# Output projection moved behind all of attention, with two levels of seven products, and projections per 512 tokens

## The chip, the cores and the metric

One core of a Trainium2 chip runs the whole kernel; the other cores are idle. The metric is the device time of one execution in microseconds (us), as a median of several runs. Everything is computed in float32.

## The reference, cut to what matters

A layer of a transformer for 1024 tokens of width 512: attention, then a feed-forward part with a small router, each between a layer norm before and a layer norm behind, with the input added again.

```python
q = (hidden_states @ w_q).reshape(B, S, Hkv, g, D)      # 512 -> 32 heads of 128
k = (hidden_states @ w_k).reshape(B, S, Hkv, D)         # 512 -> 8 heads of 128
v = (hidden_states @ w_v).reshape(B, S, Hkv, D)
scores = jnp.einsum('bqhgd,bkhd->bhgqk', q, k) * scale  # causal mask, softmax over k
attn = jnp.einsum('bhgqk,bkhd->bqhgd', probs, v)
return attn.reshape(B, S, Hq * D) @ w_o                 # 4096 -> 512
...
x = x + _layernorm(_L0_attn_ref(_layernorm(x), ...))
x = x + _layernorm(_L0_ffn_ref(_layernorm(x), ...))
```

The feed-forward part multiplies by a 512 x 512 base matrix, and by eight small matrices of rank 16 that are weighted by a softmax over 15 routes.

## The kernel before, in words

Tokens are cut into 8 row tiles of 128 (`t` from 0 to 7). The 8 key heads are 8 groups (`g`), each with 4 query heads (R). A **block** is one (g, t), 64 in all; the list `blocks` (lines 88 to 92) sets their order: for groups 0 to 5 t from 0 to 7, while the last two groups go in turn over pairs of row tiles, in the order 0, 3, 2, 1.

One turn of the main loop (lines 1212 to 1286) is one block `i`. TensorE's order is the order in which the program issues it, four quarters a block. Each quarter has
- `scores` (line 701): the products of 32 queries x 4 heads with all keys up to the diagonal, into one of two PSUM buffers `s`. VectorE adds the mask and takes the minimum (line 720), ScalarE takes the exponential with its sum (735), VectorE the reciprocal (745), ScalarE scales (746), VectorE turns 32 x 32 squares of the result into the tile `T` (752);
- a share of other TensorE work: the product `po` of weights and values of block i-2 (`weighted_values`, 777), the output projection of an earlier pair of blocks, and the projections of queries, keys and values that come next.

Between the turn and `po` stands `to_keys` (767): when the four quarters of `T` are there, 16 DMAs (4 heads x 4 quarters) move it into `K`, with the keys on the partitions. They are issued by SyncE, in some short blocks by SyncE and GpSimd. SyncE also issues nearly every load; a queue takes its DMAs in order.

Projections use seven products in place of eight for a 2 x 2 block product (sums of blocks by GpSimd in lines 181 to 248, merging of results by VectorE in `merge`, lines 561 and 609, and `add`, 539). Queries of a pair of row tiles (256 tokens) are 28 products of 128 columns (`project_q_halves`, 542). Keys and values of a pair are 14 each of 128 columns for two groups at once (`project_halves`, 603). The first group's queries, keys and values are partly done in full (`project_q`, `project_k`, `project_v`). In the list of groups, such a product is named by its result: `pq`, `pk`, `pv`.

The output projection of a pair (`project_o_pair`, 823) is 14 products of 256 columns, one level of seven products, added by VectorE to the running sums `acc` in SBUF (line 858) after every group. Its results are `pa` to `pe`. For the last group it is done row by row in full (`project_o`, 796, result `pO`), so that norms, router and base layer of finished rows (`ffn_norms`, `ffn_router`, `ffn_out`, 884 to 1015) fill later blocks. After the last block the rest of the rows follows in an order written out by hand (lines 1289 to 1324).

Of the kernel before, what the change touches and what calls it, by code (L numbers as in the profile page):

```python
# [10 lines left out]
I32 = mybir.dt.int32  # L11
# [11 lines left out]
def kernel(  # L23
# [17 lines left out]

# [6 lines left out]
    KC = H // P  # L63
    QB = 512
    NQB = S // QB
    TPB = QB // P
    PQ = 2 * P
# [6 lines left out]
    RANK = ER // E  # L74
    scale = float(D) ** -0.5
# [7 lines left out]
    ffn = ctx.enter_context(tc.tile_pool(name="ffn", bufs=2))  # L83
# [3 lines left out]

    pairs = [(g, u) for g in range(G - 2) for u in range(NT // 2)]
    pairs += [(g, u) for u in (0, 3, 2, 1) for g in (G - 2, G - 1)]
    blocks = [(g, 2 * u + e) for g, u in pairs for e in range(2)]  # L90
    N = len(blocks)
    N2 = (G - 2) * NT


    QL = range(N2 // 2 + 5, N // 2)
    QW = [*range(1, N2 // 2 + 4), *QL]
# [3 lines left out]

    def order(ins):

        return keep(ins)
# [9 lines left out]

    def turn_tile(kind, g, t):

        if (kind, t % 2) in long_tiles:
            return long_tiles[kind, t % 2]
        size = (NT - 1 + t % 2) * NSUB * P
        w = turn.tile([P, size], F32, tag=f"{kind}{t % 2}", name=f"{kind}_{g}_{t}")
        if (g, t) in blocks[N2 + 6 : N2 + 8]:  # L120
            long_tiles[kind, t % 2] = w
        return w

    def spare(kind, e, n):

        at = (NT - 3 + e + n) * NSUB * P
        return long_tiles[kind, e][:, at : at + NSUB * P].rearrange("p (k n) -> p k n", k=KC // 2)

    def last_sums(m):

        g, u = pairs[m]
        w = [weights["q", i][1] for i in range(2)]
        hk = KC // 2
        a11, a12, a21, a22 = w[0][:, :hk], w[0][:, hk:], w[1][:, :hk], w[1][:, hk:]
        s1, s2, s4 = spare("T", 0, 0), spare("T", 0, 1), spare("T", 1, 0)
        xp = xnT[u * PQ // QB][:, :, ts(u % (QB // PQ), PQ)]
        b11, b12, b21, b22 = xp[:, :hk, :P], xp[:, :hk, P:], xp[:, hk:, :P], xp[:, hk:, P:]
        t1, t2, t3, t4 = (spare("K", 0, n // 2)[:, :, ts(n % 2, P)] for n in range(4))
        todo = [
            (s1, a21, a22, ALU.add),  # L140
            (s2, s1, a11, ALU.subtract),
            (a21, a11, a21, ALU.subtract),
            (s4, a12, s2, ALU.subtract),
        ]
        if weights["tx of"] != u or m == QL[0]:
            todo += [
                (t1, b12, b11, ALU.subtract),
                (t2, b22, t1, ALU.subtract),
                (t3, b22, b12, ALU.subtract),
                (t4, b21, t2, ALU.subtract),  # L150
            ]
        weights["sq", 0] = (a11, a12, s4, a22, s1, s2, a21)
        weights["sq"] = (g,)
        weights["tx"] = (b11, b21, b22, t4, t1, t2, t3)
        weights["tx of"] = u
        return todo

    long_tiles = {}

    LATE = {(e, n): k for e, ks in enumerate(((0, 0, 2, 2), (4, 0, 0, 0))) for n, k in enumerate(ks)}  # L160

    weights = {}

    def load_k(g, by=nc.scalar):
        wk = wp.tile([P, KC * D], F32, tag="wk", name=f"wk_{g}")
        wk = weights["k", g] = wk.rearrange("p (c n) -> p c n", c=KC)
        load(wk, w_k[:, ts(g, D)].rearrange("(c p) n -> p c n", p=P), by)

    def scale_k(g):
        keep(nc.scalar.mul(weights["k", g], weights["k", g], scale))  # L170

    def load_q(g, i, by=nc.scalar):

        if weights.get(("q", i), (None,))[0] == g:
            return
        hw = R * D // 2
        w = wp.tile([P, KC, hw], F32, tag=f"wq{i}", name=f"wq_{g}_{i}", bufs=1)
        load(w, w_q[:, ts(2 * g + i, hw)].rearrange("(c p) n -> p c n", p=P), by)
        weights["q", i] = (g, w)

    pool_jobs = []

    def pool_off(most):

        for _ in range(min(most, len(pool_jobs))):
            pool_jobs.pop(0)()
# [4 lines left out]
    def combine_w(key, parts, sums):  # L191


        (a11, a12, a21, a22), (s1, s2, s4) = parts, sums
        for dst, p, q, op in (
            (s1, a21, a22, ALU.add),
            (s2, s1, a11, ALU.subtract),
            (a21, a11, a21, ALU.subtract),
            (s4, a12, s2, ALU.subtract),
        ):  # L200
            pool_sum(dst, p, q, op)
        weights[key] = (a11, a12, s4, a22, s1, s2, a21)

    def combine_q(m):

        g = pairs[m][0]
        if weights.get("sq", (None,))[0] == g:
            return
        w = [weights["q", i][1] for i in range(2)]
        hk = KC // 2  # L210
        parts = w[0][:, :hk], w[0][:, hk:], w[1][:, :hk], w[1][:, hk:]
        sums = [
            ffn.tile([P, hk, 2 * D], F32, tag="hy", name=f"sq_{g}_{n}", bufs=3) for n in range(3)
        ]
        combine_w(("sq", 0), parts, sums)
        weights["sq"] = (g,)

    def combine_k(g):

        w = [weights["k", n] for n in (g, g + 1)]  # L220
        hk = KC // 2
        two = ffn.tile([P, 2, hk, D], F32, tag="hT", name=f"sk_{g}")
        kv = ffn.tile([P, KC, NR + ER], F32, tag="skv", name=f"skv_{g}", bufs=1)
        kv = kv.rearrange("p c n -> p (c n)")[:, : 2 * hk * D]
        kv = kv.rearrange("p (x c n) -> p x c n", x=2, c=hk)
        weights["skv"] = kv[:, 1]
        parts = w[0][:, :hk], w[0][:, hk:], w[1][:, :hk], w[1][:, hk:]
        combine_w(("sk", g), parts, (two[:, 0], two[:, 1], kv[:, 0]))

    def combine_v(gv):  # L230

        hk = KC // 2
        two = ffn.tile([P, 2, hk, D], F32, tag="hT", name=f"sv_{gv}")
        w = [weights["v", gv, i * hk, "half"] for i in range(2)]
        parts = w[0][:, :, :D], w[1][:, :, :D], w[0][:, :, D:], w[1][:, :, D:]
        combine_w(("sv", gv), parts, (two[:, 0], two[:, 1], weights.pop("skv")))

    def combine_x(u, m):

        hk = KC // 2  # L240
        xp = xnT[u * PQ // QB][:, :, ts(u % (QB // PQ), PQ)]
        b11, b12, b21, b22 = xp[:, :hk, :P], xp[:, :hk, P:], xp[:, hk:, :P], xp[:, hk:, P:]
        t12, t34 = (ffn.tile([P, 2, hk, P], F32, tag="x", name=f"tx_{u}_{m}_{n}") for n in range(2))
        t1, t2, t3, t4 = t12[:, 0], t12[:, 1], t34[:, 0], t34[:, 1]
        for dst, p, q in ((t1, b12, b11), (t2, b22, t1), (t3, b22, b12), (t4, b21, t2)):
            pool_sum(dst, p, q, ALU.subtract)
        weights["tx"] = (b11, b21, b22, t4, t1, t2, t3)
        weights["tx of"] = u

    def load_v(gv, i, by=nc.scalar):  # L250

        w = wp.tile([P, KC // 2 * GV * D], F32, tag="wv", name=f"wv_{gv}_{i}")
        w = w.rearrange("p (c n) -> p c n", c=KC // 2)
        rows = w_v[ts(i, KC // 2 * P), ts(gv, GV * D)]
        load(w, rows.rearrange("(c p) n -> p c n", p=P), by)
        weights["v", gv, i * (KC // 2), "half"] = w
        for c in range(KC // 2):
            weights["v", gv, i * (KC // 2) + c] = w[:, c, :]

    def load_o(g, by=nc.scalar):  # L260
        wo = wp.tile([P, R, H], F32, tag="wo", name=f"wo_{g}")
        for j in range(R):
            load(wo[:, j, :], w_o[ts(g * R + j, P), :], by)
        weights["o", g] = wo

    def load_base(tag, cs, by=nc.scalar):
        for c in cs:
            w = weights["base", c] = wp.tile([P, H], F32, tag=tag, name=f"wbase_{c}")
            load(w, base_wt[ts(c, P), :], by)

# [13 lines left out]
    load_k(0, nc.sync)  # L284
    for i in range(2):
        load_q(0, i, two[1 - i])
    for t in range(TPB, NT):
        load(x_in[:, t, :], x[ts(t, P), :])

    ident = const.tile([P, P], F32, tag="ident", name="ident")  # L290
    make_identity(nc, ident)
    diag = ffn.tile([P, P], F32, tag="hwT", name="diag")
    neg_half = const.tile([P, 1], F32, tag="neg_half", name="neg_half")
    nc.gpsimd.memset(neg_half, -0.5)

    xnT = [big.tile([P, KC, QB], F32, tag=f"xnT{b}", name=f"xnT_{b}") for b in range(NQB)]


    hn = H // 2
    sums_o = [big.tile([P, 5, hn], F32, tag=f"acc{u}", name=f"acc_{u}") for u in range(NT // 2)]  # L300
    acc = [
        sums_o[t // 2][:, 1 + 2 * (t % 2) : 3 + 2 * (t % 2), :].rearrange("p a n -> p (a n)")
        for t in range(NT)
    ]


    late = {}
# [27 lines left out]

    def prepare_map():

        emap_f = const.tile([P, NR], F32, tag="emap_f", name="emap_f")
        keep(nc.vector.tensor_copy(emap_f, emap_i))
        for e in range(E):  # L340
            keep(
# [1024 lines left out]
```

## Time and profile before

| what | value |
|---|---|
| median of 3 runs | 1051.4 us (1051.25 to 1052.24) |
| the profiled execution, its own time | 1052.36 us |
| span of its records | 1050.6 us |
| mean granted TensorE clock | 0.999 |
| transfers | 112.02 MB in 79668 packets, mean 107 GB/s |
| `K<-T` transfers issued by SyncE | 969 (507, 589, 1847 ns to issue: least, median, most) |
| `K<-T` from issue to landing | 1.7, 2.1, 6.3 us (least, median, most) |

How to read it: the profile has busy time, count and mean duration for groups of instructions by line, engine and tile; PE is TensorE, DVE VectorE, ACT ScalarE, POOL GpSimd, SP SyncE; SPq is SyncE's issuing of DMAs. A group is named "result <- operands". Helpers record the instructions, so all products stand under line 106 and are told apart by their tiles. In a row of the timeline the columns are start, duration, engine, line, operation, tiles, shapes and how many were merged. A row by windows has the window, its length, then busy time and count for TensorE, its weight load, VectorE, ScalarE and GpSimd, the granted clock, the share of the DMA engines' time and GB/s.

### The profile page before, as it was taken

To read this page: it belongs to the slowest core of one execution; us is meant where nothing else is said; L and a number is where in the kernel's file an instruction comes from. 1 tells how busy PE (TensorE), PEld (TensorE's weight loads), DVE (VectorE), ACT (ScalarE), POOL (GpSimd) and SP (SyncE) were. 2 spreads that over 40 slices of the span, in tenths; PEclk is the share of its full clock that TensorE was granted. 3 is DMA by queue.
4 is the path that set the end of the run, shared out by engine and by line. 5 is a ranking of instruction groups with operands and counts; after the bars stand their busy time and mean duration, and the time that the engine had idled before them with its cause. 6 is when DMAs were issued, how large, how long until landed. Compare 5 with 4: busy or idle time off the path is not lost.

```text
span 1050.6 us, 16002 instructions
## 1 busy us (share of the span) xinstructions
PE 1042.0 (99%) x4974; PEld 736.8 (70%) x4974; DVE 720.8 (69%) x1855; ACT 471.9 (45%) x962; POOL 287.8 (27%) x524
## 2 busy tenths in 40 slices
PE   9999999999999999999999999999999999999997
PEld 7876677767787677667787667767788555666554
DVE  4676557776577766776477765876567867577676
ACT  2654435553344544554245444654234654444422
POOL 5413015341030214341031312542162112333112
PEclk9999999999999999999999999999999999999999
DMA  5145332653125352453314442464332773543331
GB/s 190 32 126 146 71 91 71 169 150 85 26 55 161 92 122 67 117 153 79 76 51 122 109 108 69 128 171 118 86 108 89 180 183 91 141 120 92 83 97 41
DMA packets 79668, 112.02 MB, mean 107 GB/s; under 512 B 18704, under 2 KB 51200, under 8 KB 79584
## 3 DMA queue, kind: packets, MB, share of 16 engines
q1 hardware_dynamic: 76592, 106.79, 39.2%
q0 software_dynamic: 1904, 2.90, 1.2%
q10 hardware_dynamic: 1088, 1.31, 0.4%
q8 instruction: 40, 0.66, 0.3%
q14 instruction: 44, 0.36, 0.1%
HBM read 33.34 MB, written 2.10 MB: 34 GB/s over the span
## 4 chain that ended last, share of the span: by engine, by line
PE 97%; DVE 1%; ACT 1%; issue 1%; POOL 0%; DVEq 0%; ACTq 0%; POOLq 0%
PE po L106 23%; PE s L106 21%; PE pq L106 19%; PE pv L106 5%; PE pk L106 5%; PE pe L106 5%; PE pa L106 5%; PE pf L106 3%; PE pO L106 3%; PE pb L106 2%; PE pc L106 2%; PE pd L106 2%; PE pl L106 1%; PE idle L109 1%; DVE s L720 0%
## 5 line engine op out<-in xcount | busy, mean ns | idle before, releaser
L746 ACT ACTIVATE p<-p,rec 128x32 f32<-128x32 f32 (+31 forms) x256 | 188.2, 735 | 269.6 <-DVE rec L745 269.5
L106 PE MATMUL po<-K,v 128*128 128x512 f32 x576 | 279.7, 594 | 0.3
L106 PE MATMUL s<-kT,qT 128*128 128x512 f32 (+15 forms) x768 | 272.0, 463 | 0.0
L752 DVE STREAM_TRANSPOSE T<-p 128x128 f32<-128x128 f32 (+7 forms) x256 | 198.3, 776 | 64.8 <-ACT p L746 49.5
L720 DVE CUSTOM_DVE_ANT_0 s<-s,smask 128x32 f32<-128x32 f32 (+31 forms) x256 | 180.3, 704 | 88.4 <-PE s L106 87.9
L735 ACT ACTIVATE p<-s,nmax 128x32 f32<-128x32 f32 (+31 forms) x256 | 178.9, 699 | 129.2 <-DVE nmax L720 126.6
L106 PEld LDWEIGHTS s<-kT,qT 128*128 128x128 f32 x768 | 140.0, 190 | 111.0 <-issue 100.7
L699 POOL MEMSET p<- 128x96 f32 (+2 forms) x192 | 29.1, 152 | 537.9 <-DVE T L752 492.1
L106 PEld LDWEIGHTS po<-K,v 128*128 128x128 f32 x576 | 103.7, 190 | 59.4 <-issue 50.4
L540 DVE TENSOR_TENSOR qT<-pq,qT 128x256 f32<-128x256 f32 x180 | 80.2, 461 | 44.9 <-ACT qT L566 24.9
L106 PEld LDWEIGHTS pq<-xnT,wq 128*128 128x128 f32 x544 | 71.5, 192 | 9.0 <-issue 6.4
L106 PE MATMUL pq<-xnT,wq 128*128 128x128 f32 (+1 forms) x544 | 75.5, 287 | 0.0
L783 ACT COPY attnT<-po 128x512 f32<-128x512 f32 x64 | 37.3, 582 | 72.4 <-PE po L106 72.4
L106 PEld LDWEIGHTS pq<-tx,sq 128*128 128x128 f32 x432 | 55.9, 192 | 7.2 <-issue 6.9
L106 PEld LDWEIGHTS pq<-tx,wq 128*128 128x128 f32 x432 | 55.0, 192 | 7.9 <-issue 7.5
L106 PE MATMUL pq<-tx,sq 128*128 128x128 f32 x432 | 60.1, 275 | 0.0
L106 PE MATMUL pa<-wo,attnT 128*128 128x256 f32 x224 | 58.5, 385 | 0.0
L106 PE MATMUL pq<-tx,wq 128*128 128x128 f32 x432 | 57.5, 275 | 0.0
L106 PEld LDWEIGHTS pa<-wo,attnT 128*128 128x128 f32 x224 | 41.1, 190 | 14.1 <-issue 9.3
L735 ACT ACTIVATION_READ_ACCUMULATOR p<-s,nmax 128x1 f32 x256 | 49.5, 193 | 0.0
L189 POOL TENSOR_TENSOR tx<-xnT 128x256 f32<-128x256 f32 x54 | 39.6, 734 | 19.6 <-PE pv L106 11.8
L112 POOL DMA_DIRECT2D K<-T x55 | 27.4, 504 | 54.1 <-PE s L106 22.7
(176 smaller groups left out, 1343.5 us busy)
## 6 DMA issues: line engine op xcount, KB each, us to landing
K<-T SPq DMA_DIRECT2D x128, 128.0 KB, 2.4
K<-T SPq DMA_DIRECT2D x128, 112.0 KB, 2.3
wq<-in_w_q_dram SPq DMA_DIRECT2D x27, 512.0 KB, 4.8
K<-T SPq DMA_DIRECT2D x128, 96.0 KB, 2.2
K<-T SPq DMA_DIRECT2D x128, 80.0 KB, 2.1
wo<-in_w_o_dram SPq DMA_DIRECT2D x32, 256.0 KB, 4.4
K<-T SPq DMA_DIRECT2D x108, 64.0 KB, 2.0
K<-T SPq DMA_DIRECT2D x113, 48.0 KB, 2.0
```

The costliest lines, as they stand in the source:

```text
L106: keep(nc.tensor.matmul(*args, **kw))
L109: keep(nc.tensor.transpose(*args))
L112: keep(by.dma_start(dst, src))
L189: pool_jobs.append(lambda: keep(nc.gpsimd.tensor_tensor(dst, p, q, op)))
L540: nc.vector.tensor_tensor(dst, src, to, ALU.add)
L699: keep(nc.gpsimd.memset(p[:, t * P + (j + 1) * SQ : (t + 1) * P], 0.0))
L720: nc.vector.tensor_tensor_reduce(out=s[:, :n], in0=s[:, :n], in1=smask[:, S - n :], scale=-1.0, scalar=-MASKED, op0=ALU.add, op1=ALU.min, ...
L735: keep(nc.scalar.activation(p[:, :n], s[:, :n], AF.Exp, bias=nmax, scale=-1.0, accum_out=total))
L746: keep(nc.scalar.mul(p[:, :n], p[:, :n], rec))
L752: nc.vector.transpose(turned[g, t][:, :, j, :, :].rearrange("p b k q -> p k b q"), p[:, :full].rearrange("p (k b q) -> p k b q", b=R, q=SQ),)
L783: copy = nc.scalar.copy(o, po)
```

## The change

Most functions are touched. What it does:

- **Order.** Blocks go group by group, t from 0 to 7, for all 8 groups. No output projection, norm or router runs between them.
- **Projections per 512 tokens.** `project_q_halves` now covers 512 tokens with 28 products of 256 columns, `project_k_halves` 512 tokens with 14 of 256, `project_v_halves` 512 tokens with 28 of 128. They are cut over the four blocks of a half group by the weights `SHARES`: during t=0 to 3 the values or next keys and the second half's queries, during t=4 to 7 the same for the other half and the next group's first queries. The last group has no projections in its second half.
- **Short blocks through device memory.** For t under 3 (`BOUNCED`) the turned tile is stored with one DMA, and in the next block four DMAs read it into `K`. For t of 3 and over there are 16 DMAs, all by SyncE.
- **Attention kept in device memory.** `po` of a pair goes to a tile with room for seven operands; VectorE makes four sums (`pair_sums`), and one DMA stores all seven operands (`pair_store`, 917 KB) to `attn_d`. GpSimd makes four sums of the output weights, also stored (`wo_d`).
- **Output projection behind the last block.** Seven outer products, each over all 8 groups in 4 chunks; a chunk is read back (1.0 MB of attention, 0.5 MB of weights), VectorE and GpSimd make four sums each, and TensorE runs 28 products of 128 columns: seven inner products, two groups, two column halves. Results stay in four PSUM banks for a whole outer product, then `merge_inner` and `merge_outer` put the 1024 x 512 result together. Chunks 0 and 1 are fetched in the block before the last, later chunks three ahead.
- **Rows.** Norms of row tiles 0, 2, 4, 6 start in the sixth outer product, router and base layer of 0 and 2 run inside the last; the four odd row tiles and the rest follow by an order written out by hand.

```diff
+    blocks = [(g, t) for g in range(G) for t in range(NT)]
...
+            matmul(
+                pm[n][:, :, ts(c, SQ)],
+                weights["sq", g][i][:, k, ts(c, D)],
+                weights["tx", a][i][:, k, :].rearrange("p (s q) -> p s q", q=SQ),
...
+    def to_keys(g, t):
+        w = turned.pop((g, t))
+        k = keyed[g, t] = turn_view(turn_tile("K", g, t), t)
+        if t < BOUNCED:
...
+            load(d, w[:, :size])
+            d = d.rearrange("(h q) (b n) -> b q h n", h=R, b=NSUB)
+
+            def arrive():
+                for b in range(NSUB):
+                    load(k[ts(b, SQ)].rearrange("q h s k n -> q h (s k n)"), d[b])
...
+        src = turn_view(w, t)
         for h in range(R):
             for b in range(NSUB):
+                load(k[ts(b, SQ), h], src[ts(h, SQ), b])
...
+    def pair_store(m):
+        g, u = divmod(m, NT // 2)
+        at = pair_tiles.pop((g, u)).rearrange("p n h q -> p n (h q)")
+        load(attn_d[:, g, :, ts(u, 2 * P)].rearrange("n p q -> p n q"), at)
...
+            matmul(
+                banks_o[n][m // 2][:, m % 2, r],
+                a[i][:, k, r, :],
+                w[i][:, k, :],
+                start=first,
+                stop=last,
+            )
...
+        return [
+            (cost(P), lambda k=k, m=m, r=r: piece(k, m, r))
+            for k in range(GC)
+            for m in range(7)
+            for r in range(2)
+        ]
...
+    SHARES = ((5.5, 4.9, 4.2, 3.7), (5.2, 4.8, 4.3, 4.0))
...
+        pv = attend(i - 2) if i >= 2 else []
+        parts = cut(weave(fill.pop(0), pv), [1] * NSUB)
         for n in range(NSUB):
+            scores(g, t, n)
+            run(parts[n])
+            if n == 1:
+                arrive()
+                if i % 2 == 0 and i >= 4:
+                    pair_sums(i // 2 - 2)
+            if n == 3 and i % 2 == 0 and i >= 4:
+                pair_store(i // 2 - 2)
...
+            if i == N - 2 and n == 2:
+                fetch(0)
+                fetch(1)
...
+    def begin_chunk(k):
+        if k == 1:
+            pair_sums(N // 2 - 1)
+            pair_store(N // 2 - 1)
+            fetch(3)
+        if 1 <= k and k + 3 < LAST:
+            fetch(k + 3)
+        if k + 2 < LAST:
+            chunk_sums(k + 2)
...
+    for k in range(LAST - NCH):
+        begin_chunk(k)
+        run(chunk_products(k))
+        if k == 0:
+            run(attend(N - 1))
```

## The prediction

> **What bounds the kernel now.** I read the page first: engine totals, the chain that ended last, then TensorE's waits.
>
> ```profile
> PE 1042.0 (99%) x4974; PEld 736.8 (70%) x4974; DVE 720.8 (69%) x1855; ACT 471.9 (45%) x962; POOL 287.8 (27%) x524
> ...
> PE 97%; DVE 1%; ACT 1%; issue 1%; POOL 0%; DVEq 0%; ACTq 0%; POOLq 0%
> ...
> L106 PE MATMUL po<-K,v 128*128 128x512 f32 x576 | 279.7, 594 | 0.3
> ```
>
> TensorE is busy for 1042 of 1050.6 us, and the only waits of its products that the list of waits names are 2.3 and 0.4 us. So time is the sum of TensorE's products, and a change gains by fewer of them and loses by every wait it makes. 576 records for 288 products of `po` (36 a group, 8 groups): each f32 product is two records. Their mean, 594 ns, contains a pipeline; the price is the distance from start to start, from the timeline of TensorE:
>
> ```profile
> 412.91 1.95 PE L106 MATMUL pq<-xnT,wq 128*128 128x128 f32 x16
> 414.69 0.39 PE L106 MATMUL pq<-tx,sq 128*128 128x128 f32 x2
> ...
> 1007.02 1.03 PE L106 MATMUL pc<-wot,attnT 128*128 128x256 f32 x4
> 1007.88 1.03 PE L106 MATMUL pd<-wo,sums 128*128 128x256 f32 x4
> ...
> 1014.70 3.60 PE L106 MATMUL pO<-wo,attnT 128*128 128x512 f32 x8
> 1018.13 3.60 PE L106 MATMUL po<-K,v 128*128 128x512 f32 x8
> ```
>
> 16 records of 128 columns take 414.69 - 412.91 = 1.78 us, 0.1113 each; of 256, (1007.88 - 1007.02) / 4, about 0.216 (the mean over many such pairs); of 512, 3.43 / 8 = 0.429. One of 128 is 0.003 dearer than half of one of 256.
>
> **The change on TensorE.** Records before and after:
> - Queries: 30 projections of 28 products, 128 wide: 1680 x 0.1113 = 187.0 us. After: 15 of 28, 256 wide: 840 x 0.216 = 181.4. Gain 5.6. (The two written out in full stay.)
> - Keys: 336 x 0.1113 + 32 x 0.429 = 51.1; after, 7 x 14 products of 256 and 8 of 512: 196 x 0.216 + 16 x 0.429 = 49.2. Gain 1.9.
> - Values: 336 x 0.1113 + 64 x 0.216 = 51.2; after, 7 x 28 products of 128 and 16 of 256: 392 x 0.1113 + 32 x 0.216 = 50.5. Gain 0.7.
> - Output: 28 pairs x 14 products of 256, and 32 of 512 for the last group: 784 x 0.216 + 64 x 0.429 = 196.8. After: 7 x 7 products over everything, as 28 chunks of 28 products, but only 128 wide: 1568 x 0.1113 = 174.5. Gain 22.3.
>
> Together 30.5 us. If nothing waited, the profiled execution of 1052.4 us would become 1021.9.
>
> **What no longer covers.** 197 us of output products leave the attention blocks. They were what TensorE did while a block's weights travelled. That journey is the row tile's turned `T`, cut into 16 transfers into `K`, and the product `po` two blocks later needs all 16. I followed one in the timeline of VectorE (first the next block's first mask operation, then the last turn of t=7), then a whole set of 16 on SyncE's timeline, then the page's list of transfers:
>
> ```profile
> 621.84 0.18 DVE L720 CUSTOM_DVE_ANT_0 s<-s,smask 128x32 f32<-128x32 f32 x1
> ...
> 623.19 1.25 DVE L752 STREAM_TRANSPOSE T<-p 128x1024 f32<-128x1024 f32 x1 [1.12 <-ACT p L746]
> ```
>
> ```profile
> 820.94 10.09 SPq L112 DMA_DIRECT2D K<-T  x16
> ```
>
> ```profile
> K<-T SPq DMA_DIRECT2D x128, 128.0 KB, 2.4
> ```
>
> The turn ends 623.19 + 1.25 - 621.84 = 2.6 us after the next block's first mask operation; the 16 issues then take 16 x 0.63 = 10.1 us, the last starting about 9.5 us on; it lands 2.4 us after its start. So `K` of t=7 is ready 14.5 us after the next block begins; by the smaller turns and landings 13.4 for t=3 and t=4, 14.0 for t=5 and 6. Before, blocks average 1042 / 64 = 16.3 us and all this is covered.
>
> After, I add a block from its products (scores by width, `po` of two blocks back, and its share of the half's projections, 18.2 us cut 5.5 : 4.9 : 4.2 : 3.7, then 5.2 : 4.8 : 4.3 : 4.0):
> - t=0: 0.9 + 14 x 0.429 + 5.5 = 12.4 us. `po` of t=7 wants its keys 0.4 us into the next block, at 12.8; ready at 14.5. **Wait 1.7**, in six groups: 10.2.
> - t=4: 4.3 + 2.6 + 5.2 = 12.1; `po` of t=3 wants them at 12.8, ready at 13.4. Wait 0.6 x 6 = 3.6 (group 0 has longer blocks).
> - t=5, 6, 7: 13.0, 14.3, 15.7: no wait. t=0 to 2 go through device memory instead, as 5 issues: 1.4 (turn) + 2.3 (a 128 KB store lands in 1.7, a 256 KB one in 3.0, the rows of `out_dram`) + 4 x 0.55 + 2.0 = 8 us, against blocks t=2 and 3 of 7.3 and 8.5 us and a first `po` some 0.9 us in. Hidden, by under 1.5 us; a landing of 4 us there costs 2 a group.
> - VectorE in t=2: 2.0 + 1.2 + 2.2 (mask, reciprocal and accumulator reads, turns) + 4 x 0.42 for the four sums that feed the second level + 1.7 for merges, 8.7 us by durations, some 7.4 as they overlap, against TensorE's 7.3. A stretch at 88% VectorE cost TensorE 0.4 us:
>
> ```profile
> 820.00:840.00 20.00, 19.59 (x49) 8.89 (x48) 17.69 (x34) 13.81 (x20) 2.85 (x7) 1.00 0.78 192
> ```
>
> I take 0.5 a group, 3.5 in all; between 0 (two score buffers absorb it) and 1.4 x 7 = 10.
>
> **The last group** has no next group to project: 12.1 us of queries in its first half, nothing in its second. Block t=0 falls to 10.5 us, so `po` of the group before waits 3.7. Blocks t=2 to 4 lose 1.7 (VectorE, and the journey through device memory). Block t=4 lasts 8.0, so `po` of t=3 waits 13.4 - 8.2 = 5.2; after it SyncE has not finished one tile's 16 issues when the next tile is turned, and t=4 and t=5 wait 2.0 each. 14.6 together. Bounds: 8 (issues at 0.51, the shortest seen) to 22 (each transfer a microsecond later).
>
> **Handover, 5 us.** Reads of chunks 0 and 1 (3 MB) are queued ahead of `K` of t=6: 3.0. `K` of t=7 is ready 4.2 + 9.5 + 2.4 = 16.1 us after the last block; `po` of t=6 and one chunk cover 15.2: 1. Chunk 3 needs that `po`, four sums, a store and a 1.5 MB read, about 13 us, and its own sums; two chunks cover 12.5: 1. Bounds 1 to 12.
>
> **The last stage.** A chunk is 56 records x 0.1113 = 6.23 us and reads 1.57 MB, 252 GB/s. The first 20 us moved 250 GB/s with the DMA engines 73% busy, so 342 full; the stretch above 192 at 78%, so 246. At 246 a chunk takes 6.4 us and 28 lose 4.7; I take 0, since these are device-memory reads in long rows, nearer to the first. VectorE's sums (4 x 0.68 us) and GpSimd's (4 x 0.73) lie under a chunk; product results alternate between two sets of banks. After the last chunk four row tiles still need two norms, router and base layer each, and two more most of it: 37 us on TensorE, VectorE 5.1 + 37; the chain at its ends makes it 3.5 longer than now. The start: 1 for the first sums on GpSimd.
>
> **Sum:** 1052.4 - 30.5 + 10.2 + 3.6 + 3.5 + 14.6 + 5 + 3.5 + 1 = 1063.3 us; the median of the runs is 1.0 below the profiled execution, so 1062.
>
> [...]
> The trace begins with 26 idle products in 5.81 us, 223 ns each, twice the 111 of later. [...]
>
> **Rivals.**
> - **The journey is covered, and it is faster: 1039.** Place: `po` of t=7 and t=3 in every group. It decides from the point where 16 issues take 8.1 us (the 0.507 us minimum) and not 9.5 to 10: then the 13.8 of t=7 and t=3 go, with VectorE's 3.5, and some 6 of the last group: 1052.4 - 30.5 + 18 - 1. For it: issues of 0.51 exist. Against: the median is 0.59 and whole sets take 10.
> - **The transfers get in each other's way: 1083.** The stage carries 29 MB of attention stores and 8 of weight sums more in less time. If each journey is 1 us longer (landings of `K` reach 6.3 us against a median of 2.1), t=3, 4 and 7 wait 1 more in seven groups: 1062 + 21. Against: DMA share rarely passes 0.7.
> - **The second level does not give its saving:** products of 128 with a new stationary tile each cost 0.122 and not 0.111 (the 143-wide `pl` records): 1568 x 0.011 = 17, so 1079. Against: the `pq` records change it too.
>
> **How the numbers follow.** Forecast 1062 (1050 to 1074): 0.52. Rival one (1028 to 1050): 0.30. Rivals two and three: 0.18. What lies within 0.2% of 1051.4, 1049.3 to 1053.5, cannot be told from no change: 0.08, from the borders of the first two. Faster 0.28, slower 0.64. The range leaves out a tenth at each end: 1037 to 1083.
>
> **What would show it.** In the profile after: TensorE's busy time near 1012 with idle time by `po`, ended by DMA `K<-T`, 10 to 20 us before the last group; its idle share largest in one stretch of some 50 us around 800; 128-wide records 0.111 apart in the last stage with no waits for `oa`. Wrong if `po` never waits for `K` (then rival one), or if the last stage waits for reads.

## The result, and the profile after

The changed kernel takes **1208.6 us** (median of four runs, 1206.7 to 1211.8) against 1051.7 of the kernel before, a ratio of 1.1495 [1.1468, 1.1522]. The forecast was 1062, some 10 us more than before, with a range up to 1083: the sign was right, the size, 157 us, far off. The profiled execution has a span of 1209.9 us and a mean granted clock of 0.943.

From the page of the changed kernel: engine totals and the group of `po`.

```profile
PE 1068.5 (88%) x4722; PEld 746.1 (62%) x4722; DVE 756.4 (63%) x1740; ACT 478.1 (40%) x946; POOL 284.4 (24%) x492
...
L81 PE MATMUL po<-K,v 128*128 128x512 f32 x576 | 312.6, 631 | 84.8 <-DMA K<-turned 29.1
```

TensorE has 252 records fewer and yet 26 us more busy time: a record is longer where the clock is halved (one of 512 columns takes 1.06 us there and 0.59 at full clock, in the median). `po`, with 0.3 us of idle time before, now has 84.8. The list of TensorE's waits (total us, times, longest):

```profile
PE po L81 <- DMA K<-turned: 29.1, 7, 6.2
PE po L81 <- DMA K<-T: 22.5, 10, 5.2
PE ptx_h L84 <- DVE om L783: 19.4, 1, 19.4
PE po L81 <- ACT at L651: 14.9, 7, 2.3
PE pf L81 <- ACT hwT L949: 14.1, 3, 6.8
PE po L81 <- ACT p L589: 8.6, 4, 4.0
PE pl L81 <- ACT hT L276: 7.7, 3, 4.1
PE po L81 <- ACT p L598: 7.1, 5, 2.6
...
PE po L81 <- issue: 2.5, 1, 2.5
```

Every wait of `po` over 0.3 us stands ahead of the first product of a tile, and those that the list puts down to ScalarE's `p` or to "issue" (18.2 us) end 0.2 to 0.5 us after the last transfer into `K` has landed. So they are waits for keys too: 69.8 of the 84.8 us are for keys, and 14.9 (`ACT at`) are for the bank of `po`. By the row tile whose keys were missing, the 69.8 are 31.2 for t=2, 15.6 for t=7, 9.7 for t=4, 7.7 for t=3, 5.2 for the last t=6 and 0.4 for one t=1.

**Where the time went.** I priced every record of TensorE at the distances of the prediction (0.1113, 0.216 and 0.429 us). The kernel before has 1035.7 us of such work, the changed one 1005.3. What the span has above that is loss, cut here at the first mask operation of each group:

```
stretch                    length   work at full clock   loss
start and group 0           129.9        119.2           10.7
groups 1 to 6               666.9        579.1           87.8   (109 to 113 us a group, 96.5 of work)
group 7                     105.2         71.0           34.2
last stage, 28 chunks       235.0        199.3           35.7
row tiles behind it          72.9         36.8           36.1
```

204.5 us of loss in all, against 14.9 before: 189.6 more, less 30.4 of work, is the 159 us between the two spans. The 87.8 us of groups 1 to 6 are 45.1 of waits for keys, 14.9 for the bank, and 27.8 left over; TensorE ran at half clock for 47 us there, which is worth some 23 of them.

**A wait for keys, read through.** It is the `po` of t=2, in block t=4 of group 3. SyncE's timeline ahead of it (start, duration, engine, line, operation, tiles, how many merged):

```profile
387.24 0.38 SPq L87 DMA_DIRECT2D attn_d<-at  x1
387.67 1.78 SPq L87 DMA_DIRECT2D wv<-in_w_v_dram  x2
390.70 0.34 SPq L87 DMA_DIRECT2D turned<-T  x1
398.01 1.75 SPq L87 DMA_DIRECT2D K<-turned  x4
399.86 0.38 SPq L87 DMA_DIRECT2D wo_d<-wot  x1
```

TensorE's timeline and the rows by windows say what happened beside it (after the engines' busy time and counts: clock, share of the DMA engines, GB/s):

```profile
404.37 2.05 PE L81 MATMUL po<-K,v 128*128 128x512 f32 x2 [6.17 <-DMA K<-turned]
```

```profile
390.00:397.00 7.00, 7.00 (x25) 4.23 (x23) 6.23 (x15) 5.45 (x13) 0.45 (x3) 1.00 0.99 258
397.00:404.00 7.00, 1.20 (x7) 0.75 (x5) 3.00 (x7) 2.27 (x4) 0.12 (x1) 0.77 0.75 179
```

The store of the turned tile is issued at 390.70, but 1.4 MB of attention and value weights were issued just ahead in the same queue, and the DMA engines are full (0.99). Only at 398.01 can SyncE issue the reads: 7.3 us for a store that the prediction gave 2.3. The four reads take until 404.3, 6.3 us where it gave 4.2, and TensorE has stood still for 6.17 us; its first records afterwards are at half clock (the two above take 2.05 us, two at full clock 1.12, at 463.71).

### The profile page after: what moved, and what is told of

It reads as the page before. It is cut to its first block, busy times and chain, and to the rows that moved or that the text cites. A ratio compares the mean times of both kernels' runs of the same rounds, so it can differ in the third digit from the quotient of the medians.

```text
span 1209.9 us, 14998 instructions
## 1 busy us (share of the span) xinstructions
PE 1068.5 (88%) x4722; PEld 746.1 (62%) x4722; DVE 756.4 (63%) x1740; ACT 478.1 (40%) x946; POOL 284.4 (24%) x492
## 5 line engine op out<-in xcount | busy, mean ns | idle before, releaser
L81 PE MATMUL po<-K,v 128*128 128x512 f32 x576 | 312.6, 631 | 84.8 <-DMA K<-turned 29.1
L81 PEld LDWEIGHTS o<-ow,oa 128*128 128x128 f32 x1176 | 138.2, 197 | 8.2 <-issue 4.3
L81 PE MATMUL o<-ow,oa 128*128 128x128 f32 x1176 | 139.5, 280 | 3.6 <-POOL ow L736 2.2
L730 DVE TENSOR_TENSOR oa<-oa 128x512 f32<-128x512 f32 x112 | 103.3, 966 | 21.8 <-DMA oa<-attn_d 14.6
L736 POOL TENSOR_TENSOR ow<-ow 128x256 f32<-128x256 f32 x84 | 78.3, 952 | 73.9 <-DMA ow<-in_w_o_dram 51.9
L81 PE MATMUL pq<-xnT,wq 128*128 128x256 f32 x304 | 82.7, 387 | 0.0
L410 DVE TENSOR_TENSOR qT<-pq,qT 128x512 f32<-128x512 f32 x90 | 68.8, 765 | 16.4 <-PE pq L81 16.1
L597 DVE RECIPROCAL rec<-total 128x1 f32<-128x1 f32 x256 | 39.4, 154 | 58.9 <-ACT p L589 56.8
L81 PEld LDWEIGHTS pq<-xnT,wq 128*128 128x128 f32 x304 | 58.3, 195 | 25.8 <-issue 19.4
L674 DVE TENSOR_TENSOR at<-at 128x256 f32<-128x256 f32 x128 | 56.4, 482 | 18.9 <-ACT at L651 17.8
L81 PE MATMUL pq<-tx,sq 128*128 128x256 f32 x240 | 64.9, 383 | 0.0
L81 PE MATMUL pq<-tx,wq 128*128 128x256 f32 x240 | 63.1, 379 | 0.0
```

Of the source, the lines that this page charges most:

```text
L81: keep(nc.tensor.matmul(*args, **kw))
L410: pinned(nc.vector.tensor_tensor(dst, src, to, ALU.add))
L597: keep(nc.vector.reciprocal(rec, total))
L674: keep(nc.vector.tensor_tensor(dst, p, q, op))
L730: keep(nc.vector.tensor_tensor(dst, p, q, op))
L736: keep(nc.gpsimd.tensor_tensor(dst, p, q, ALU.subtract))
```

## The experiments

**1. The big transfers on another queue.** In the changed kernel the stores of attention and weight sums and the loads of weights are issued by ScalarE:

```diff
-        load(attn_d[...].rearrange("n p q -> p n q"), at)
+        load(attn_d[...].rearrange("n p q -> p n q"), at, nc.scalar)
...
-                load_q(g + 1, i)
+                load_q(g + 1, i, nc.scalar)
```

> Theory A (the journey of short blocks through device memory stands in SyncE's one queue behind the big stores and loads): with the attention stores, the weight-sum stores and the weight loads issued by ScalarE, the wait of po for K<-turned (29 us in 7 waits) goes, and with it some 15 us of half clock behind those waits: about 1165 us, between 1155 and 1180. Rival B (the 16 issues of a tile on SyncE set the waits, as I forecast): SyncE is relieved of some 12 of 150 issues a group only, so 1200 to 1210. Rival C (the DMA engines are simply full, whatever the queue): the waits stay or move to K<-T, 1195 to 1215.

Measured: 1287.9 us, ratio 1.225 [1.220, 1.230], so 79 us slower than the change itself and above all three forecasts. TensorE's waits, and two stretches by windows around one of them (block t=3 to t=4 of group 3, 12 us of waiting):

```profile
PE po L81 <- DMA K<-T: 94.8, 19, 12.5
PE po L81 <- DMA K<-turned: 24.6, 4, 9.5
```

```profile
420.00:428.00 8.00, 8.00 (x29) 4.90 (x28) 6.37 (x19) 5.54 (x13) 0.42 (x3) 1.00 1.02 265
428.00:434.00 6.00, 0.91 (x4) 0.46 (x3) 3.40 (x7) 2.51 (x5) 0.17 (x2) 0.75 0.96 276
```

A second queue did not clear the way for the keys. By the row tile, `po` waited 70.5 us for t=2 (31.2 in the changed kernel) and 49.8 for t=7 (15.6). In the stretch shown the DMA engines were full (1.02, 0.96), and the four reads of the tile of t=2 landed after 8.0 us in the median, not 3.9. That fits their sharing the engines with transfers that had stood behind them in SyncE's one queue. How much of it came from ScalarE's own work standing behind its DMAs was not separated.

**2. The single bank of `po` out of the way.** `po` has one PSUM bank, and in block t=0 the product waited for ScalarE's copy of the one before. A quarter of the block's projections is put ahead:

```diff
+        own = fill.pop(0)
+        head = len(own) // 4 if t == 0 else 0
-        parts = cut(weave(fill.pop(0), pv), [1] * NSUB)
+        parts = cut(own[:head] + weave(own[head:], pv), [1] * NSUB)
```

> In the first block of a group the first quarter of the projections now runs ahead of the first po. Theory A (the single PSUM bank of po waits there for ScalarE's copy of the po before, 2.1 to 2.4 us in seven places, and the clock halves for 3.4 us behind each): 15 us of waits and about 12 of half clock go: about 1182 us, between 1178 and 1190. Rival (VectorE and ScalarE bound these blocks, the wait only shows where TensorE meets them): the time moves to other waits, 1200 to 1212.

Measured: 1217.5 us, 1.158 [1.1546, 1.1613], above both forecasts. The wait for the copy fell from 14.9 to 6.1 us, but the wait for keys rose from 22.5 to

```profile
PE po L81 <- DMA K<-T: 47.4, 15, 5.9
```

Most of that is at the next `po`, one block later: that of t=7 waited 31.7 us for its keys in all, 15.6 in the changed kernel. A wait was exchanged, not removed.

**3. The norms of rows 2, 4, 6 one step per chunk.** In the changed kernel all four steps of a row tile's norms stand in one chunk.

```diff
-            go(t, t, t, t)
+            go(*range(t, -1, -2))
...
+        if k < LAST - 1:
+            work += act_now(*range(6, 2 * (k - (LAST - NCH)), -2))
```

> The norms of the even row tiles go one step a chunk, so that VectorE no longer stands still for GpSimd and ScalarE within a step. Theory A (VectorE falls 4 us a chunk behind over four chunks, and the merge that frees the banks comes 19 us late): the wait of 19.4 us goes, and part of the half clock behind it: 1180 to 1190 us. Rival (VectorE has too much work in this stage in any order): the wait goes by less than half, or the odd row tiles behind take the time back: over 1200.

Measured: 1199.5 us, 1.1409 [1.1355, 1.1463], 9.1 less than the change, between the two forecasts. The 19.4 us wait of the turn of row 0 fell to 0.3, and 7.9 of it came back one step further on (TensorE's timeline):

```profile
1074.90 0.66 PE L84 MATMUL ptx_h<-ident,h 128*128 128x128 f32 x4 [0.33 <-DVE om L783]
```

```profile
PE pl L81 <- ACT hT L276: 15.7, 4, 7.9
```

**4. Idle products in the wait of t=4**, so that the clock stays up: 40 in odd groups, 20 in even ones, on the changed kernel.

```diff
+            idle_ones = [(0, lambda n=n: keep_busy(n)) for n in range(40 if g % 2 else 20)]
+            parts[0] = parts[0][:first] + idle_ones + parts[0][first:]
```

> 40 (odd groups) or 20 (even groups) idle transposes, 4.5 or 2.2 us, stand ahead of the first po of t=4, where TensorE waits 5 to 6 or 3 us for its keys. Theory A (the wait itself costs its length, and the half clock behind it another 1.7 to 3.4 us each time): the waits only get shorter by what the idle products fill, and the half clock behind them goes: 10 to 18 us less, 1191 to 1199. Rival (the granted clock makes no difference, since other engines bound what follows): 1207 to 1213.

Measured: 1216.8 us, 1.1574 [1.154, 1.1607], above both forecasts. In groups 1 to 6 the half clock of block t=4 was gone but for group 3 (two windows of 3.4 us in place of nine), and its waits were shorter, but the time was not:

```profile
PE po L81 <- DMA K<-T: 30.8, 10, 8.9
...
PE po L81 <- DMA K<-turned: 10.3, 7, 3.1
```

What TensorE gained there it waited for later: the `po` of t=2 waited 20.9 us less, those of t=3, t=7 and the last t=6 waited 14.0 more. Groups 1 to 6 took 112 us on average, 111 in the changed kernel.

**5. No stores of attention and of weight sums.** The last stage reads as much from other matrices.

```diff
-        load(attn_d[:, g, :, ts(u, 2 * P)].rearrange("n p q -> p n q"), at)
...
-        load(raw, attn_d[A_AT[i], g0 : g0 + GC].rearrange("g p n -> p g n"))
+        load(raw, w_q[ts(i % 4, P), : 16 * P].rearrange("p (g n) -> p g n", g=GC))
```

> Leaves out the stores of the attention operands (32 of 0.9 MB) and of the weight sums (16 of 0.5 MB); the last stage reads the same amounts from w_q and w_o instead, so its output products are made from other numbers. Theory B, the one in-order queue of SyncE bounds the attention groups by issuing 16 transfers at 0.6 us each and by standing still while a store of T lands: the two stores a pair cost SyncE little, groups stay within 4 us of 112, time 1180 to 1210. Theory C, the volume that is queued ahead of the keys bounds them: 37 MB less, at 250 to 340 GB/s 110 to 150 us of transfer time less over eight groups; each store of T lands some 3 us sooner, groups fall to about 102 us, TensorE's waits for K<-turned and the half clock behind them go, time 1110 to 1150. Either way the last stage stays at about 235 us.

Measured: 1165.1 us, 1.108 [1.1061, 1.110], 43.5 less. This lies between the theories' numbers. Groups 1 to 6 take 105.6 us each, not 111. The store of the turned tile of t=2 (768 KB) and of t=0 (256 KB) lands sooner, first in the changed kernel's list of transfers, then in this one's:

```profile
turned<-T SPq DMA_DIRECT2D x8, 768.0 KB, 5.2
...
turned<-T SPq DMA_DIRECT2D x8, 256.0 KB, 7.5
```

```profile
turned<-T SPq DMA_DIRECT2D x8, 768.0 KB, 3.3
...
turned<-T SPq DMA_DIRECT2D x8, 256.0 KB, 3.2
```

`po` waited 14.3 us for the keys of t=2, not 31.2, but as long as before for those of t=7 (15.9) and for its bank. So the volume queued ahead of the keys is one part. It is not all: 113 us are left.

**6 and 7. Two issuers for the keys; no way through device memory.** Number 6 lets GpSimd issue every second transfer for t of 3 and over; number 7 does that for all row tiles, with no row tile going through device memory.

```diff
-    BOUNCED = 3
+    BOUNCED = 0
...
-                load(k[ts(b, SQ), h], src[ts(h, SQ), b])
+                load(k[ts(b, SQ), h], src[ts(h, SQ), b], (nc.sync, nc.gpsimd)[b % 2])
```

> For row tiles 3 to 7, every second of the 16 transfers of T into K is issued by GpSimd and not by SyncE; nothing else. Theory B (SyncE's issuing and its standing still bound the groups): the 16 issues take some 5 us in place of 10, waits of TensorE for K<-T fall from 22 us to under 5, those for K<-turned by half, groups fall from 112 to about 103, time 1135 to 1165. Theory C (volume ahead of the keys): the transfers land when the DMA engines have room for them, groups stay within 3 us of 112, time 1190 to 1210. A third way, as with ScalarE as second queue: the transfers of the two queues hold each other up, time above 1215.

> No way through device memory for row tiles 0 to 2: all eight row tiles go from T to K in 16 transfers each, every second one issued by GpSimd. 11.8 MB less in stores and as much less in reads. Theory B: SyncE no longer stands still until a store of T has landed (109 us of its waits), 8 issues a queue take 5 us; waits of TensorE for K fall to under 10 us in all, groups to about 100, time 1100 to 1140. Theory C: the volume falls by a tenth, groups fall by 2 to 4 us, time 1170 to 1195. If the way through device memory was worth its place, short blocks wait longer than before for 16 issues: time above 1210.

Measured: number 6 1185.5 us (1.1293 [1.1262, 1.1323]), number 7 1162.9 (1.1051 [1.1032, 1.1070]). Both lie between the theories' numbers. In number 6 the wait for K<-turned stayed at 29.8 us; in number 7 it is gone, with SyncE's 108.6 us of standing still until a store of `T` has landed, and a group takes 105 us. But its list has 35.2 us of waits for K<-T, more than the 22.5 of the changed kernel and far from the "under 10" of theory B: for t=7, `po` waited 27.0 us. Its landings are slower, which fits more transfers being on their way at a time: 128 KB in 3.9 and 5.1 us in place of 2.4.

```profile
K<-T SPq DMA_DIRECT2D x64, 128.0 KB, 3.9
K<-T POOLq DMA_DIRECT2D x64, 128.0 KB, 5.1
```

**8. The clock by itself, on the kernel of number 7.** Idle products in the two waits that were left in nearly every group, 27 in t=1 and 20 in t=4 of odd groups.

> The kernel of e7_no_bounce (no way through device memory, every second transfer into K issued by GpSimd; 1162.9 us), and in groups 1 to 7 idle products in the two places where TensorE waited for K in nearly every group there: 27 (3.0 us) ahead of the first product of po in block t=1, and 20 (2.2 us) ahead of it in block t=4 of odd groups. They take the place of waits of 2 to 3 us, each of which has a stretch of 3.4 us at half clock behind it. Theory D, the half clock is a loss of its own: some eleven stretches of 3.4 us at half clock go, 1.7 us each, time 1140 to 1148. Theory E, the groups' period is set by the journeys and not by TensorE, so that what TensorE saves it waits for later (as in e4_keep_busy): time 1158 to 1170.

Measured: 1152.0 us, 1.0951 [1.0934, 1.0968], 10.9 less, between the two forecasts. Of the eleven windows of 3.4 us at half clock that groups 1 to 6 had, nine are gone, and these groups are 8.9 us shorter in the profiles. So the half clock is a loss of its own, some 1.0 to 1.2 us a window and not 1.7; that fits a part of each window being the wait itself, in which the clock loses nothing (in the changed kernel TensorE stood still in 42 of 137 us at half clock). With the keys' way shortened by number 7, what number 4 could not get is got.

**9. GpSimd's sums of the last stage left out.**

```diff
-        for dst, p, q in ((t1, b12, b11), (t2, b22, t1), (t3, b22, b12), (t4, b21, t2)):
-            keep(nc.gpsimd.tensor_tensor(dst, p, q, ALU.subtract))
```

> The changed kernel, but in the last stage GpSimd's four sums of the output weights per chunk are left out; the inner products read the raw quarters in their place, so the result is made from other numbers. Theory F, VectorE and GpSimd slow each other on SBUF operands: VectorE's sums of oa fall from a mean of 0.97 to about 0.68 us, it no longer falls behind in chunks 20 to 23, the wait of the turn of row 0 for om falls from 19.4 us to under 6, and the 20 us at half clock behind it go; time 1180 to 1190. Theory G, VectorE falls behind because of the round trips of the norms alone: the sums get no shorter, the wait stays above 15 us, time above 1200.

Measured: 1202.0 us, 1.1438 [1.1419, 1.1457], 6.6 less. VectorE's sums, first in the changed kernel, then without GpSimd beside them (busy, mean ns of one | idle time before):

```profile
L730 DVE TENSOR_TENSOR oa<-oa 128x512 f32<-128x512 f32 x112 | 103.3, 966 | 21.8 <-DMA oa<-attn_d 14.6
```

```profile
L730 DVE TENSOR_TENSOR oa<-oa 128x512 f32<-128x512 f32 x112 | 72.0, 686 | 40.8 <-DMA oa<-attn_d 30.5 <-DMA ow<-in_w_o_dram 9.3
```

```profile
PE ptx_h L84 <- DVE om L781: 14.1, 1, 14.1
```

The mechanism is there, 0.28 us a sum, but the 19.4 us wait fell only to 14.1: most of it is the chain of the norms (experiment 3), not the sums.

**10. The cover put back.** 28 idle products in each of 60 blocks of the changed kernel, 60 x 28 x 0.111 = 187 us.

```diff
+            def cover(n):
+                spare = bank(f"spare_{i}_{n}")
+                for k in range(KC):
+                    transpose(spare[:, ts(k, P)], ident, ident)
+
+            mixed = weave(mixed, [(KC * cost(P), lambda n=n: cover(n)) for n in range(7)])
```

> The changed kernel with 28 idle products (3.1 us) woven into each of 60 blocks of attention, 187 us in all: about as much as the output projection had there before. Theory H, the waits in attention are there because that cover was taken away: the waits for K nearly vanish, the half clock with them, a group goes from 112 us to its 96.4 of TensorE work plus 24.9, 121 us, and the time rises by far less than the 187 us added: 1280 to 1300. Theory I, the waits come from the journey's own resources (the queue, the DMA engines) and would be there with any filling: they stay, and the time rises by 160 to 190: 1370 to 1395.

Measured: 1287.1 us, 1.2246 [1.2227, 1.2264]. 187 us of work cost 78. Group 3 by windows, and the waits that are left:

```profile
378.60:499.80 121.20, 121.20 (x564) 84.27 (x563) 70.75 (x171) 55.10 (x109) 17.21 (x40) 1.00 0.61 152
```

```profile
PE po L81 <- DMA K<-T: 13.4, 3, 8.7
...
PE po L81 <- DMA K<-turned: 0.6, 1, 0.6
```

Groups 1 to 6 have no loss at all: 121 us, all of it work, clock 1.00, with the same stores and issues. This decides the main question: the waits are there because the output products that covered them were taken away. Queue and volume (5 to 7) are part of what sets how long the way is. Three fillings of the same kernel fit a way of some 111 us a group: 96.5 us of work took 111, some 100 (experiment 4) took 112, 121 took 121; before, groups 1 to 5 took 121. The way itself was not summed step by step. It is not the issuing alone, since SyncE also stands still until VectorE has turned a tile, as the changed kernel's list of its waits shows:

```profile
SPq L87 <- DVE T L604: 116.0, 34, 7.0
SPq L87 <- DMA turned<-T: 108.6, 24, 7.0
```

**11 and 12. What helps, together.** Number 11 joins 3 and 8; number 12 adds idle products in six places of the last rows.

> e8_no_bounce_busy (1152.0 us) and e3_norms_stepwise in one kernel: keys without the way through device memory and issued by SyncE and GpSimd, idle products in the waits of t=1 and t=4, and the norms of rows 2, 4, 6 spread over the last outer product. If the losses of attention and of the last stage are independent, the 9.1 us of e3 come off whole: 1140 to 1146. If the norms' spread helps only because something else was late in attention, 1148 to 1154. By either it is still slower than before, since some 30 us are lost in the last group and 35 behind the last chunk.

> e11_together, and idle products in five waits of the last rows: 60 ahead of the router's products of row tile 0, 32 of row tile 4, 20 of the row tile c (1), and 45, 18 and 50 ahead of the last products of the base layer of 4, 6 and d (3). No wait gets shorter by it; only the clock stays up. In e3_norms_stepwise 37 us from 1081 on run at half clock. Theory D, the half clock there delays products on the path that sets the end: 6 to 12 us less than e11_together. Theory J, the path there is the chain of VectorE, ScalarE and GpSimd, and TensorE's products lie in its slack: within 3 us of it.

Measured: 1137.4 us (1.0813 [1.0789, 1.0836]) and 1131.6 (1.0757 [1.0739, 1.0775]). Number 11 is 14.6 below number 8, more than the 9.1 expected; number 12 is 5.8 below 11, just under the 6 to 12 that the clock was to give. The best version of the changed kernel is still 7.6% slower than the kernel before.

## Why the prediction was wrong, point by point

- **The gain on TensorE: right.** 30.5 us by my count, 30.4 by the records. The 128-wide products of the last stage kept their distance: 125.00 us for 1120 records is 0.1116, so rival three is out; its 0.122 came from records 143 columns wide, which their width alone gives (0.1113 x 143 / 128 = 0.124).

```profile
950.00:1075.00 125.00, 125.00 (x1120) 125.00 (x1120) 96.71 (x134) 5.37 (x8) 79.00 (x84) 1.00 0.81 289
```

- **"Hidden, by under 1.5 us": the step that failed first.** I gave the store of the turned tile 2.3 us from landings of transfers that nothing stood ahead of, 128 and 256 KB. The tiles are 256, 512 and 768 KB, and 0.9 MB of attention and weights were issued ahead of them: 7.5, 2.7 and 5.2 us. The text had the price of it ("a landing of 4 us there costs 2 a group"), but I had not looked at what SyncE issues before it. Cost: 25.8 us of waits for the keys of t=2 in groups 1 to 6, 31.2 in all, and the half clock behind them. The slow store of t=0 cost no wait.
- **Waits at t=7 and t=3, 13.8:** place and size were right: 10.4 and 4.7 us ahead of the last group, where I had 10.2 and 3.6. Not seen: 4.2 for t=4 in the same groups.
- **The half clock, priced at 0: wrong.** I took a wait to cost its length and no more; that was my estimate, and the trace before, whose longest wait behind its start is 0.4 us, could not show it. The changed kernel spends some 137 us at half clock, most of it in and behind waits of 2 to 6 us and 20 at the one of 19.4. In 42 of them TensorE stood still; in the other 95 it ran at half pace (products of 512 columns 0.853 us apart, not 0.429), which is some 47 us lost. Experiments 8 and 12 got 10.9 and 5.8 us back by nothing but keeping TensorE busy.
- **The bank of `po`, not seen: 14.9 us** of waits in seven groups. It was no wait before because the output products stood between two `po`; my list of what the cover hid had only the keys on it. Experiment 2 showed that what is gained there is waited for at the next `po`.
- **VectorE in t=2, 3.5:** no wait for its mask or its merges stands in the list. This term was too high.
- **The attention groups together:** I had 17.3 us for groups 1 to 7, and it was 87.8 in six. The reasoning was block by block, each wait by itself. Of this, keys are 45.1, the bank 14.9, and the rest mostly half clock. Experiments 4 and 2 show that the sum was wrong in kind too: one queue carries keys, stores and weights in order (in the wait read through above it issued nothing from 391.0 to 398.0 us, until a store had landed), and while the keys' way is longer than the work of a group (111 us against 96.5), a wait that is taken away in one block comes back in another.
- **The last group, 14.6:** 34.2 by the table. Its waits for keys are 14.5, near my sum by luck: 5.4 of them are for t=2, which I took as hidden but for a part of 1.7, and t=3 waited 1.6, not 5.2. The rest is half clock and a wait of 4.0 us of the last block's scores: VectorE made the first chunk's sums (3.2 us) ahead of their mask.
- **"VectorE's sums (4 x 0.68 us) and GpSimd's (4 x 0.73) lie under a chunk", last stage 0, handover 5:** 35.7. Some 13 of it lie in the handover: `po` waited 5.2 and 2.2 us for the last two tiles' keys (I had 3 and 1), the first output products 3.6 for their weights and sums. With the cover of experiment 10 the first of these waits was 8.7. From 950 to 1075 us next to nothing was lost. Reads were not the limit, as I had argued (289 GB/s, 3.6 us of idle time before the products `o`). But beside GpSimd's sums VectorE's are slower (0.97 us each, 0.69 without them), and the norms of four rows go back and forth between VectorE, GpSimd and ScalarE in the same chunks; the merge that frees the PSUM banks came late, and TensorE stood for 19.4 us, with 5.5 at half clock behind it. I had checked each engine's busy time against a chunk, not the chain through them.
- **Behind the last chunk, 3.5:** by the table some 29 more than the 6.9 of loss that the end of the kernel before has. The rows wait for ScalarE's copies behind VectorE's chain (14.1 and 7.7 us), and TensorE is at half clock for 24 us of 73. The 37 us of work were right (36.8); I had kept the old end's efficiency for them.
- **Rivals.** The second (transfers in each other's way) has its mechanism shown by 5, at twice its price, 43 us and not 21. The first (the journey covered) is out: two issuers in 6 and 7 shortened the issue and gave 23 and 46 us, and covered nothing fully.

Where experiment 7's remaining 9 us a group come from is only partly settled: number 8 takes some away; group 4 has one wait of over 5 us in each of 7 and 8. In 7 it is for the keys of t=7: the transfers issued at 446.9 to 447.8 us landed 9.4 to 9.9 us later, while an attention store and a weight load issued beside them took 11.1 and 12.2, so volume is in the way there too.

## What to carry to other kernels

Before work is moved away from a stage, ask what that work covers, and sum the time of the stage's longest chain, a queue in order included, over the whole stage; as a first estimate the stage takes the larger of that and TensorE's work. Here 197 us of output products went, a group with 96.5 us of work left took 111, and a saving of 30 us became 159 us more. A wait that was removed while that chain was the longer one moved (experiment 2: 8.8 us less for the bank, 24.9 more for keys; experiment 4: 20.9 less for t=2, 14.0 more elsewhere). With the chain shortened first (7, 46 us less), the rest paid (8, 10.9).

## What the runs showed of the hardware

**Half clock came in windows of 3.413 us.** In the changed kernel's trace all 25 stretches at half clock start on one grid of that step. I summed TensorE's idle time in each of the 350 windows from 8.2 us on: what its records, at the distances of the prediction and twice that at half clock, leave of the window. After a window at full clock with up to 2.06 us of idle time the next was full in all 285 cases; with 2.13 or more it was half in all 24. After a window at half clock the next was full in the 24 cases with up to 0.68 us idle, and half in the 16 with 1.34 or more. The wait of above, window by window on that grid:

```profile
397.29:400.70 3.41, 0.91 (x4) 0.46 (x3) 2.32 (x7) 2.27 (x4) 0.12 (x1) 1.00 0.52 118
400.70:404.11 3.41, 0.00 (x0) 0.00 (x0) 0.39 (x1) 0.00 (x0) 0.00 (x0) 0.50 1.03 254
404.11:407.53 3.42, 3.16 (x5) 1.85 (x6) 0.00 (x0) 0.00 (x0) 0.00 (x0) 0.50 1.08 363
407.53:410.94 3.41, 3.41 (x15) 2.33 (x14) 2.12 (x4) 1.32 (x3) 1.24 (x1) 1.00 0.86 234
```

The first window has 2.5 us of idle time, and the second is at half clock; the second is idle, and the third is at half clock too, with slower products (2.05 us for two of `po` and not 1.12). A wait of some 2 us was free or cost a window here, by where it fell: of the seven waits for the bank, 1.95 to 2.28 us long, four have a window at half clock behind them and three have none. The four lie in one window each, but for 0.16 us of one; the three are cut by a border of the grid.

**VectorE's and GpSimd's sums on operands in SBUF were slower side by side.** Timeline of VectorE, then of GpSimd, in the changed kernel's last stage:

```profile
1075.50 4.47 DVE L730 TENSOR_TENSOR oa<-oa 128x512 f32<-128x512 f32 x4
```

```profile
1075.31 4.12 POOL L736 TENSOR_TENSOR ow<-ow 128x256 f32<-128x256 f32 x4
```

Without GpSimd four such sums of VectorE take 2.74 us (4 x 0.686, experiment 9). GpSimd's four, beside a merge that reads PSUM, took 2.90:

```profile
1050.99 2.90 POOL L736 TENSOR_TENSOR ow<-ow 128x256 f32<-128x256 f32 x4 [2.60 <-DMA ow<-wo_d]
```

One after the other would be 5.64; side by side they ended within 4.66 (spans on GpSimd are rough). So both were slowed, 4.47 us against 2.74 and 4.12 against 2.90, and still overlapped in part.

**A second issuing engine changed the order, not the room.** Two issuers for the small transfers of one tile helped (23 us in 6). Big transfers moved to a second issuer cost 79 us (1): the DMA engines moved 265 to 276 GB/s in the full stretch shown, 258 in that of the changed kernel, and the reads of keys took 8.0 us in place of 3.9. In these runs the one queue in order had kept the keys ahead of transfers that were issued later; ScalarE's part in the 79 us is open.
